# Five units' convolution taps on TensorE, floors under squared norms moved, and a new order of issue in a fused attention and expert block

## The chip, the cores and the metric

The kernel runs on 1 core of a Trainium2 chip. The metric is the device time of one execution in microseconds (us), as the median of several runs. The engines are named as the profile names them: PE is TensorE (matmuls), PEld its weight loads, DVE is VectorE, ACT is ScalarE, POOL is GpSimd, and SP is the queue from which nearly all transfers are issued.

## The reference, cut to what matters

The input `x` has 8 sequences of 512 tokens with 128 features in f32. Four sublayers follow each other, each with a layer norm before it and an addition after it:

```python
x = x + attn_a(layernorm(x))   # short convolution, delta rule, 16 heads of 8
x = x + ffn(layernorm(x))      # 8 experts, two chosen for each token   ("f")
x = x + attn_b(layernorm(x))   # linear attention with elu + 1          ("b")
x = x + ffn(layernorm(x))      # the same experts again                 ("g")

# in attn_a
q = silu(short_conv(x @ Wq.T, conv_q))      # 4 taps along the tokens; k and v alike
q, k = l2norm(q), l2norm(k)                 # x / max(sqrt(sum(x * x)), 1e-6)
v_new = (v_t - k_t S) * beta_t;  S = S + k_t v_new;  o_t = q_t S    # token by token
o = o * rsqrt(mean(o * o) + 1e-6) * o_norm_w;  out = o @ Wo.T
# in ffn
probs = softmax(x @ Wg); the two largest, divided by their sum, weigh
relu(x @ W1[e]) @ W2[e]
```

## The kernel before

**Units.** The 512 tokens are cut into eight units of 64 tokens (times 8 sequences, so 512 rows). Each unit goes through the sublayers in turn, and the units overlap. `prepare(c)` does unit c's layer norm, projections, convolution, norms and the solve of four tokens at a time; `recurring` runs the delta rule over all units, 16 steps for each, with four VectorE operations in a step (`pj`, `factors`, `terms`, `st`); POOL forms the outputs (`po`) and `ending(c)` normalizes them and sends them through DRAM (`sco`, `oT`). `moe` runs the experts for f and g, `linear_attention` and `attend` run b. In the profile the first sublayer's tiles end in `_a`, and the others in `_f`, `_b` and `_g`. "f1" below is the expert sublayer f of unit 1.

**The order.** Each part is a Python generator that yields the name of the engine that it needs next, or an event to wait for. A planner (`Weaver`) keeps a modelled clock for each engine and always lets that part issue whose work is longest behind, corrected by `FAVOURED` and by one number for each part in `OFFSETS`. What comes out is one fixed order of instructions on each engine, and each engine works strictly in that order, PE's matmuls among them. Where the planner sees a gap on PE, `keep_busy` puts bf16 matmuls into it whose result nobody reads; line 1950 issues them and the profile calls them `busy`.

**The convolution.** `TAPS_ON_PE = 4`: for units 0 to 3, `convolved(s)` (s is q, k or v) uses four f32 matmuls with weights `wc[s]` in which the taps are folded into the projection. The profile shows two matmul records for each f32 matmul. For units 4 to 7 it uses one matmul with the plain weights `wa`, a copy to `cv` and a multiplication on ACT, three `scalar_tensor_tensor` on DVE, and two small `halo` copies on POOL. The first unit of that kind also needs three small matmuls into `pl`.

**What shares a buffer.** The folded weights `wc` lie in the space of the last three experts' weights (`resident[5]` to `resident[7]`). So `loading_later_weights` must wait:

```python
if TAPS_ON_PE and e >= NE - 3:
    yield fired("projected", TAPS_ON_PE - 1, e - (NE - 3))
```

The loads of experts 5 to 7, and the matmuls that centre their first weights (`s_cw_w` in the profile), can come only after unit 3's convolution.

**Linear attention.** In `attend`, POOL forms outer products of keys and values in the one buffer `kv`; PE then sums them along the tokens (`s_pc_b`), DVE multiplies by the queries (`qs_b`) and reduces (`nd_b`).

**Routing.** `moe` finds the largest and the second largest logit with `first_of_largest`, one after the other, then `relative` computes the two weights with a tanh on ACT, then the weights go to `cb`. From there `spread` writes them to DRAM, and each expert reads its row back as `wt_xsT`, which POOL multiplies with the tokens before `s_ph` starts.

**Floors.** A squared norm is raised to at least 1e-12 directly after it is computed: on POOL in `norms_of` (units 0 to 4), on DVE in `near_norms` (k of unit 0, and units 5 to 7).

Of the kernel before, what the change touches and what calls it, by code (L numbers as in the profile page):

```python
# [19 lines left out]
P = 128  # L20
# [17 lines left out]
TURNED = 1  # L38
# [3 lines left out]
TAPS_ON_PE = 4  # L42
# [4 lines left out]
ADDED_ON_DVE = (4,5,6,7)  # L47
NEAR_NORMS = (5,6,7)
# [5 lines left out]
TURNED_IN = (0,7)  # L54
# [13 lines left out]
PASSES = ()  # L68

FAVOURED = {  # L70
    ("b", 0.0): 1475, ("b", 1.0): -605, ("b", 2.0): 408, ("b", 3.0): -1141, ("b", 4.0): 1159, ("b", 5.0):
    -397, ("b", 6.0): -3095, ("b", 7.0): -2237, ("b", 7.5): -2071, ("beside",): 1509, ("ending",): 696,
    ("f", 0): 1839, ("f", 1): 922, ("f", 2): 673, ("f", 3): -941, ("f", 4): 1648, ("f", 5): 1050, ("f", 6):
    -1587, ("f", 7): 767, ("f", 7.5): -2892, ("g", 0.0): 1576, ("g", 1.0): 901, ("g", 2.0): 357, ("g", 3.0):
    7212, ("g", 4.0): -253, ("g", 5.0): -2424, ("g", 6.0): -246, ("g", 7.0): 1986, ("g", 7.5): -2626,
    ("outputs",): 7, ("prepare", 0): -904, ("prepare", 1): -3306, ("prepare", 2): 224, ("prepare", 3):
    -1571, ("prepare", 4): -839, ("prepare", 5): -16, ("prepare", 6): 680, ("prepare", 7): -2427, ("recur",
    0): 3219, ("recur", 1): -6342, ("recur", 2): -2844, ("recur", 3): 482, ("recur", 4): -2744, ("recur",
    5): -1405, ("recur", 6): 1064, ("recur", 7): -724, ("values",): 149, None: -1498,
# [4 lines left out]
    -5735, -5206, -179, -62, -5753, 0, -6219, -6323, 29, -6838, 1464, 2372, 2338, -2, 1277, -3446, -3136,  # L84
    2417, -3137, -2112, -3119, -3650, -311, 76, 1, 3, -3, 77, -342, -7970, 977, -20, -4091, 3665, -19, 806,
    -4343, -4621, -4648, -4379, 711, 806, -5289, 1734, 1900, 1275, 623, -5269, -420, -380, -832, -1479, 50,
    -758, -790, 125, -3620, 585, -553, 237, 2322, 2064, -5521, 501, -5381, -5928, -3498, -40, 2563, 4086,
    10628, -5495, 782, 11097, 2142, 524, -2998, -175, 1440, -9862, 334, 747, 94, -5047, -6796, 307, 308,
    -1787, -402, -3506, -63, -187, 265, -2927, -6059, -6411, -6618, 0, -4528, -6371, -6553, -6091, -5056,
    263, -538, -1107, -6503, -6983, -6, -6510, -36, -961, -967, 294, 389, -6742, -8230, -142, -7747, -8737,  # L90
    -7250, -7254, -7665, -422, 1935, 282, -996, -6683, -9031, 177, 1221, 466, 360, -7342, 552, -8817, -42,
    -7371, 101, 1699, 247, 245, 186, -7410, 57, 713, -5151, 127, -91, -80, -5933, 56, -6006, -6402, 412,
    -6116, -445, 35, 2434, -4925, -4928, -4874, -938, 1079, 406, -7960, 775, 519, -186, -183, -6551, -7752,
    -7695, -8113, 429, 2079, 1870, 73, 72, 717, 130, -428, -37, 347, 2267, 385, -69, 3340, -640, -367, 165,
    -831, -1483, 0, 486, -5539, -200, -199, -399, -34, 2547, -7582, -106, -2671, 11037, 1388, 1383, 1120,
    -962, 17, -1270, -6162, -175, -5673, 211, 50, -7246, -2444, -7484, -2599, -386, 24, -1456, -1295, -1542,
    449, 95, 3319, -2490, -5181, -17, 250, 1245, 968, 926, -3459, -1, -51, -7241, -6288, -40, -5786, 456, 0,
    2, -7292, 471, -361, -79, -6239, 1121, 209, 228, 171, -490, -335, -1339, -4313, -4533, -173, -162,
    -1885, -4676, -5235, -6460, -342, -6601, -6575, 266, 235, 4646, 4647, 78, -899, -7489, 388, -348, 4,
    2051, 1488, -3366, -170, -1594, -5834, -4738, -590, -6081, 2703, 771, 806, 2101, -1052, -4471, -334,  # L100
    10046, 384, -6869, -6546, 10224, -8058, 323, -1252, 463, 8950, 0, -8361, 1480, -113, -361, -8416, -9767,
    -47, -200, -9523, 27, -8517, -60, 66, -8349, -229, -9575, -9613, 177, 0, -516, 2087, 1808, 1102, -3472,
    -3462, -3444, -261, -48, -604, -199, 8924, -1499, -2626, 0, -5333, -68, 0, -3882, -1964, 1388, 1387,
    -3692, -5022, -5065, -555, 136, 6558, 1420, 1897, 1801, 9994, 299, 277, 324, -41, 8082, 391, 7156, 7157,
    -5841, -322, -1273, -5351, 627, 9366, -2233, -2747, 1391, 674, -7825, -11438, -30, 775, 2023, 1821,
    -1660, -376, -7698, 679, -3112, 1424, -5849, 0, -55, 151, -899, 680, -7529, -8147, 148, 896, 1077, 914,
    339, 108, 425, -1456, -5019, -1472, -477, 2580, -4207, -3854, -4163, -8696, -1145, -4645, -48, -435,
    -49, -441, -2007, 528, -6603, 2721, 2590, 71, 790, 1764, 678, -1104, -11, -8403, -631, -307, -17, 8979,
    -26, 111, 125, -3643, 387, 709, -7661, -6188, -1529, 52, -267, -2256, -1638, -163, -7464, -7718, -7716,
    -1060, 1984, -7251, 341, -416, 74, 246, 826, 0, -1331, 114, -9262, 817, -794, -1132, -4670, 22, 677,  # L110
    -1102, -247, -991, 5324, 1460, 7056, -68, 22, -4777, -5911, -267, -245, 0, -5384, 611, 1441, -3227,
    -3228, 7000, -4910, -4927, 8594, 7076, 656, 8970, 534, 0, -414, -452, 8696, 199, -1793, 526, 7399,
    -2385, -2142, -2082, 703, 601, -344, 673, 889, 675, -225, 700, 0, 1159, -2605, -52, 1613, 16, -121, 10,
    3158, 128, 131, -45, -73, 1613, -6492, -6728, -6847, 1627, -162, 2762, 283, 57, -585, 605, 1, -6681,
    -6644, -7468, 1614, -1785, -6492, 3296, -2793, 740, 1374, 1438, -5170, -5140, 909, 2571, -5016, 298,
    -5165, -4644, -50, -42, -4475, 2, 294, -85, -2740, -6839, 226, 1693, -57, 3901, -15, 128, 27, -353,
    1777, -988, 548, -1117, 51, -5550, -5713, 147, 12, -34, -4251, 1589, 1915, 47, -3918, 1053, 111, -9287,
    183, -73, -1509, -1272, -1576, 1611, -436, 1, 5846, -1241, -112, 1631, -1205, 1597, 150, -2745, -3535,
    2377, 2411, 1644, 1676, -1215, 1575, -4452, 8420, 702, -792, 816, 406, 430, 763, 8525, 846, -158, 8634,
    8574, 7499, -111, 1400, 1450, 1002, 8654, -2038, 769, 762, 607, 2855, 6551, -97, -90, -87, 5399, 647,  # L120
    -2965, 11537, -1025, 26, 1690, -128, 1901, -2876, -579, -1637, -1629, 2367, 1239, 1591, 19, 1583, 1724,
    11913, 9792, -979, -5647, 234, 2469, -6345, 305, -458, 202, 495, 2179, 331, -2292, 9691, 1045, 6, 9790,
    35, -5846, 323, 577, 1291, 9691, -58, -97, 118, -5, -4, 615, -5886, 76, -98, -106, -3895, 613, 2012,
    -4473, 833, 614, 2011, -59, -171, -3273, -3336, -3353, -3, -4885, 1032, 10012, 4, 9990, -8535, 13, -26,
    -426, 9852, -8409, 100, -8705, 1140, -1782, -3, -354, -197, -1938, -335, 9717, -197, 9802, 2602, -4020,
    6594, -4069, 2798, 3058, 2, -79, -78, 391, 1966, 1709, 200, 8716, 1885, 10615, 11418, 3662, 9797, 2272,
    1035, 2099, 0, 1824, 10195, 9823, 10532, 9755, 10009, 1333, 1142, -251, 8119, 297, 296, 41, 749, 4723,
    747, 1875, 2107, 724, -124, 453, 7278, 3607, 3799, 273, 3441, 3113, -3692, -398, -3768, -334, -3765,
    -3766, -582, -412, 9876, -382, 1211, 10712, -1001, 93, -1201, 9799, -302, 9584, 9796, 780, 9701, -580,
    1068, 9799, -828, -878, 2215, 2732, -4744, 3104, 2677, 2684, 2623, 238, -387, -153, 2284, -614, 2072,  # L130
    231, 2027, -4996, -71, 30, 457, -4797, 384, -249, 4030, 2190, -5523, 4173, 1217, 3083, 1929, -714, 605,
    676, -732, -321, -57, 3956, 733, 11526, -7059, -800, 1502, 239, -723, -808, -318, -541, 8037, -8544, 15,
    -4952, -5089, -5252, -4993, 2029, -304, -831, -5698, -69, -6182, -350, -409, 2461, 257, -282, -7155,
    -5747, 0, -11360, 2325, 2107, 2122, 386, -5700, -3106, -1352, 0, 0, -1541, 372, -1538, -3081, -1573,
    -1435, -66, 3013, -2727, -4066, -895, -131, -4357, 2917, -4077, -498, 0, -3157, -80, -404, -3201, -3374,
    0, 1576, 1292, 11286, -3695, -3696, 11437, 2265, 10445, 11425, 0, 3814, -3061, -6147, -44, -59, 400,
# [331 lines left out]
def duration(key, op, args, kw):  # L468
# [12 lines left out]
    if key == "ACT":  # L481
        table = TABLE_OF.get(args[2]) if op == "activation" else None
        scale = args[2] if op == "mul" else kw.get("scale", 1.0)
        more = (0.19 if "bias" in kw else 0.0) + (0.0 if isinstance(scale, float) else 0.08)
        return key, 0.2 + more + n * 0.76e-3, 0.1, table
# [1523 lines left out]
```

## Time and profile before

| what | value |
|---|---|
| median of 3 runs | 792.27 us (791.22 to 794.27) |
| the profiled execution | 790.81 us, span 789.1 us |
| PE busy | 758.7 us, 96% of the span |
| of that, `busy` matmuls (line 1950) | 52.7 us in 195 |
| DVE, ACT, POOL busy | 560.8, 504.7 and 446.0 us |

A PE that is busy is not always doing useful work: the `busy` matmuls count as busy. In a list of instructions or of a chain the first two numbers are the start and the duration in us. In a table of stages, each engine's busy time in the stage is followed by its number of instructions; the last three columns are the granted PE clock as a share of full speed, the share of time in which the DMA engines moved data, and GB/s.

### The profile page before, as it was taken

What the parts mean: (1) busy time and instruction counts of PE and PEld (TensorE: products, weight loads), DVE (VectorE), ACT (ScalarE), POOL (GpSimd) and SP (SyncE); (2) the same over time, 40 slices, a digit from 0 to 9 for tenths busy, and PEclk for the clock granted to TensorE, in tenths of its full rate; (3) what the DMA queues carried; (4) which work ended last, traced back from release to release, by engine and by line L of the source; (5) the groups of instructions that cost most, each with busy time, mean ns of one, the idle gap of its engine ahead of it and who ended that gap; (6) DMA issues with size and microseconds to landing.
All of it is one profiled execution on the core that took longest, in us unless ns stands there. A gap on an engine that the chain in (4) does not pass through costs nothing.

```text
span 789.1 us, 11578 instructions
## 1 busy us (share of the span) xinstructions
PE 758.7 (96%) x3383; PEld 384.7 (49%) x3383; DVE 560.8 (71%) x1429; ACT 504.7 (64%) x1388; POOL 446.0 (57%) x609
## 2 busy tenths in 40 slices
PE   8888899997999999999999999999999999999997
PEld 4344454553435434544444435453444456644475
DVE  1689898978997698899999799798557145342310
ACT  5765767688877865678676875773664445643352
POOL 1244447659586495775586664877736606735331
PEclk9999899998999999999999999999999999999999
DMA  1451426105233311214132132232112211321121
GB/s 46 118 133 42 123 63 183 45 23 148 69 97 80 98 56 55 81 55 126 54 111 96 34 102 78 82 106 67 42 41 81 60 28 48 108 69 44 37 60 34
DMA packets 82392, 59.67 MB, mean 76 GB/s; under 512 B 48152, under 2 KB 64152, under 8 KB 82328
## 3 DMA queue, kind: packets, MB, share of 16 engines
q1 hardware_dynamic: 81608, 58.64, 25.8%
q8 instruction: 27, 0.44, 0.2%
q10 hardware_dynamic: 720, 0.28, 0.2%
q14 instruction: 37, 0.30, 0.1%
HBM read 46.52 MB, written 12.39 MB: 75 GB/s over the span
## 4 chain that ended last, share of the span: by engine, by line
PE 78%; DVE 11%; ACT 6%; issue 2%; DMA 2%; POOL 1%; SPq 0%; DVEq 0%; ACTq 0%; POOLq 0%
PE s_ph_f L454 14%; PE y_py_f L454 13%; PE s_ph_g L454 13%; PE y_py_g L454 12%; PE s_pc_b L454 5%; PE s_pp_a L454 4%; PE s_pp_b L454 2%; PE busy L1950 2%; PE s_pu_b L454 2%; DVE st L454 2%; PE s_pS_b L454 2%; DVE W L454 1%; ACT squares L454 1%; DVE pj L454 1%; DVE terms L454 1%
## 5 line engine op out<-in xcount | busy, mean ns | idle before, releaser
L454 ACT ACTIVATE hT_g<-s_ph_g 128x512 f32<-128x512 f32 (+1 forms) x144 | 79.0, 552 | 95.5 <-PE s_ph_g L454 94.5
L454 PE MATMUL y_py_f<-hT_f,resident 128*128 128x512 f32 (+1 forms) x288 | 134.3, 555 | 0.3 <-ACT hT_f L454 0.2
L454 PE MATMUL s_ph_f<-wt_xsT_f,resident 128*128 128x512 f32 (+1 forms) x288 | 132.1, 554 | 1.9 <-POOL wt_xsT_f L454 1.1
L454 PE MATMUL y_py_g<-hT_g,resident 128*128 128x512 f32 (+1 forms) x288 | 133.3, 553 | 0.3
L454 PE MATMUL s_ph_g<-wt_xsT_g,resident 128*128 128x512 f32 (+1 forms) x288 | 131.0, 553 | 0.3 <-POOL wt_xsT_g L454 0.2
L454 ACT ACTIVATE hT_f<-s_ph_f 128x512 f32<-128x512 f32 (+1 forms) x144 | 78.7, 550 | 50.9 <-PE s_ph_f L454 49.4
L454 POOL TENSOR_TENSOR wt_xsT_g<-wt_xsT_g,xn_xnT_g 128x512 f32<-128x512 f32 (+1 forms) x69 | 79.0, 1166 | 37.0 <-DMA wt_xsT_g<-scw_g 26.7
L454 POOL TENSOR_TENSOR po<-st,kq 128x256 f32<-128x256 f32 x128 | 93.8, 763 | 3.3 <-DVE st L454 2.7
L454 POOL TENSOR_TENSOR kv_b<-ph_b,v 128x1152 f32<-128x1152 f32 x32 | 69.2, 2176 | 39.8 <-ACT v L454 27.1
L454 POOL TENSOR_TENSOR wt_xsT_f<-wt_xsT_f,xn_xnT_f 128x512 f32<-128x512 f32 (+1 forms) x69 | 79.4, 1168 | 17.5 <-DMA wt_xsT_f<-scw_f 17.4
L454 DVE TENSOR_TENSOR qs_b<-s_pc_b,ph_b 128x360 f32<-128x360 f32 (+1 forms) x96 | 50.4, 551 | 46.2 <-PE s_pc_b L454 45.5
L454 PEld LDWEIGHTS y_py_f<-hT_f,resident 128*128 128x128 f32 x288 | 50.6, 190 | 47.2 <-issue 40.4
L454 PEld LDWEIGHTS s_ph_f<-wt_xsT_f,resident 128*128 128x128 f32 x288 | 50.4, 190 | 47.4 <-issue 31.6
L454 PEld LDWEIGHTS y_py_g<-hT_g,resident 128*128 128x128 f32 x288 | 50.9, 190 | 44.1 <-issue 35.6
L454 PEld LDWEIGHTS s_ph_g<-wt_xsT_g,resident 128*128 128x128 f32 x288 | 50.9, 190 | 43.7 <-issue 32.0
L454 DVE TENSOR_REDUCE st<-terms 128x64 f32<-128x320 f32 x128 | 61.4, 480 | 12.3 <-ACT terms L454 6.0
L454 DVE TENSOR_REDUCE factors<-pj 128x32 f32<-128x288 f32 x128 | 58.4, 456 | 6.2 <-ACT factors L454 2.5
L1950 PE MATMUL busy<-ones 128*128 128x512 bf16 x195 | 52.7, 411 | 9.5 <-ACT o L454 3.4
L454 DVE TENSOR_TENSOR pj<-st,factors 128x256 f32<-128x256 f32 x128 | 53.4, 417 | 4.7 <-ACT factors L454 1.8
L454 DVE TENSOR_TENSOR terms<-factors,kt 128x256 f32<-128x256 f32 x128 | 53.7, 419 | 4.2 <-ACT vn L454 1.1
L454 ACT COPY terms<-st 128x64 f32<-128x64 f32 x128 | 39.6, 309 | 25.0 <-DVE st L454 23.8
L454 POOL TENSOR_TENSOR pq<-y_a,y_a 128x128 f32<-128x128 f32 x32 | 21.1, 685 | 46.2 <-ACT squares L454 23.1
(270 smaller groups left out, 1336.1 us busy)
## 6 DMA issues: line engine op xcount, KB each, us to landing
wt_xsT_f<-scw_f SPq DMA_DIRECT2D x55, 256.0 KB
wt_xsT_g<-scw_g SPq DMA_DIRECT2D x55, 256.0 KB
scr<-y_a SPq DMA_DIRECT2D x24, 256.0 KB
qk<-scr SPq DMA_DIRECT2D x16, 256.0 KB
x_a<-in_x_dram SPq DMA_DIRECT2D x16, 128.0 KB
vv<-scr SPq DMA_DIRECT2D x8, 256.0 KB
sco<-on SPq DMA_DIRECT2D x8, 256.0 KB
oT<-sco SPq DMA_DIRECT2D x8, 256.0 KB
```

The costliest lines, as they stand in the source:

```text
L454: r = call(*args, **kw)
L1950: nc.tensor.matmul(pt, ones, ones.unsqueeze(1).to_broadcast([P, 4, P]), start=True, stop=True)
```

## The change

The change has these parts:

1. The folded taps lie in the buffer `kv` of the outer products, and `TAPS_ON_PE` goes from 4 to 5. Experts 5 to 7 no longer wait for unit 3. Instead, the first unit's `attend` waits until unit 4's convolution matmuls are done before it takes `kv`.
2. Unit 4 uses 12 f32 matmuls for its taps in place of three matmuls and the ACT, DVE and POOL operations. The three `pl` matmuls move to unit 5.
3. The floor under q's squared norm goes into the operation of `ending` that adds the mean square, with `max` in the place of `mult` and the scales changed around it. The floor under k's norm in `near_norms` moves behind the square root in `back`. Five operations of POOL and seven of DVE go, and four of DVE come.
4. `relative` is started as soon as the second largest logit is known, beside the search for its place.
5. Unit 0's denominators of b lie in PSUM, in one of the five general banks.
6. The planner: other estimated durations, ten more planning passes (`PASSES`), new `FAVOURED` and `OFFSETS`. All engines get another order of instructions.

Other new branches (`STATES_ON_PE`, `KEYS_ON_POOL`, `QUERIES_ON_POOL`) are switched off by empty tuples. `TURNED` is written in another way and says the same as before.

```diff
-TAPS_ON_PE = 4
+TAPS_ON_PE = 5
+BURST = NE - 3
...
-PASSES = ()
+PASSES = ((1, 0.0, {}), (9, 0.1, {}))
...
 FAVOURED = {
...
 OFFSETS = (
...
@@ duration
-        more = (0.19 if "bias" in kw else 0.0) + (0.0 if isinstance(scale, float) else 0.08)
+        more = (0.1 if "bias" in kw else 0.0) + (0.0 if isinstance(scale, float) else 0.06)
         return key, 0.2 + more + n * 0.76e-3, 0.1, table
     if key == "POOL" and ALU.pow in args:
-        return key, 1.05, 0.1
+        return key, 0.4 + n * 0.16, 0.1
     if key == "POOL":
-        return key, 0.2 + n * (1.72e-3 if n > 512 else 2.0e-3), 0.1
+        if op == "tensor_copy":
+            return key, 0.16 + n * 1.3e-3, 0.1
+        return key, 0.18 + n * (1.73e-3 if n > 512 else 2.15e-3), 0.1
...
@@ merged
-    wc = [resident[NE - 3 + s].rearrange("p (k d) -> p k d", k=4) for s in range(3)]
+    kv_ = const.tile([P, 2, NH, V1, HD], F32, name="kv")
+    taps = kv_.rearrange("p w h e d -> p (w h e d)")[:, 0 : 12 * D].rearrange("p (s k d) -> p s k d", s=3, k=4)
+    wc = [taps[:, s] for s in range(3)]
...
-    kvs = held_in(1, [P, 2, NH, V1, HD], "kv")
+    kvs = Slots(weaver, None, None, "kv", 1, [kv_])
...
@@ loading_later_weights
-            if TAPS_ON_PE and e >= NE - 3:
-                yield fired("projected", TAPS_ON_PE - 1, e - (NE - 3))
...
                 sp.dma_start(resident[e][:, to], by)
+                if e >= BURST and to.stop < 2 * NF:
+                    weaver.moves(-LANDS)
...
@@ norms_of
-            yield "POOL" if CLAMP_ON_POOL else "DVE"
-            (pool if CLAMP_ON_POOL else dve).tensor_scalar(
-                nrm[:, s], nrm[:, s], ATT_A_EPS * ATT_A_EPS, None, ALU.max
-            )
+            if s:
+                yield "POOL"
+                pool.tensor_scalar(nrm[:, s], nrm[:, s], ATT_A_EPS * ATT_A_EPS, None, ALU.max)
...
@@ near_norms
-            yield "DVE"
-            dve.tensor_scalar(nrm[:, s], nrm[:, s], ATT_A_EPS * ATT_A_EPS, None, ALU.max)
...
@@ back
             act.activation(ri, nrm[:, 1], AF.Sqrt, scale=4.0)
+            if c == 0 or c in NEAR_NORMS:
+                yield "DVE"
+                dve.tensor_scalar(ri, ri, 2.0 * ATT_A_EPS, None, ALU.max)
...
@@ ending
-        act.activation(so, o, AF.Square)
+        act.activation(so, o, AF.Square, scale=(ATT_A_EPS * HD * HD) ** -0.5)
...
-        dve.scalar_tensor_tensor(rms, nrm[:, 0], ATT_A_EPS * HD * HD, rms, ALU.mult, ALU.add)
+        dve.scalar_tensor_tensor(rms, nrm[:, 0], ATT_A_EPS * ATT_A_EPS, rms, ALU.max, ALU.add)
...
-        act.activation(rms, rms, AF.Sqrt, scale=1.0 / HD)
+        act.activation(rms, rms, AF.Sqrt, scale=ATT_A_EPS * HD)
...
@@ moe
+        def relative(m1, m2):
...
+        def first_of_largest(p, k):
+            m = near(nb) if k else row(f"m{k}")
+            yield "DVE"
+            dve.tensor_reduce(m, p, AX.X, ALU.max)
+            if k:
+                scales["weights"] = spawn(relative(m1, m))
...
-        m2 = yield from first_of_largest(lg2, 1)
...
-        yield from relative()
+        yield from first_of_largest(lg2, 1)
+        yield scales["weights"]
...
@@ attend
         adding = spawn(elus())
+        if c == 0:
+            yield from all_of([fired("projected", TAPS_ON_PE - 1, s) for s in range(3)])
         kv = yield from kvs.take(n)
...
-        dn = yield from dns.take(n)
-        if c > 0:
+        if c == 0:
+            of_dn = yield from banks.take(f"dn_{n}")
+            dn = of_dn[:, 0 : 2 * NH].rearrange("p (i h) -> p i h", i=2)
+        else:
+            dn = yield from dns.take(n)
...
```

## The prediction

> **What bounds the kernel now.** I read the page's first two parts, then PE's time by stages, then the chain that ended last around the one stage that loses time, then the timeline and the single tiles.
>
> ```profile
> span 789.1 us, 11578 instructions
> PE   8888899997999999999999999999999999999997
> PEclk9999899998999999999999999999999999999999
> ```
>
> PE is full from about 200 us to the end and granted full speed there, except in the last slice. The other engines never come near. But a busy PE may be running `busy` matmuls, so I take four stages, first with all instructions, then line 1950 alone:
>
> ```profile
> 0.00:123.00 123.00, 108.92 (x527) 57.43 (x528) 91.15 (x242) 80.27 (x236) 46.11 (x95) 0.97 0.35 92
> 123.00:200.00 77.00, 68.74 (x326) 37.24 (x325) 65.26 (x153) 60.96 (x182) 56.20 (x84) 0.96 0.33 93
> 200.00:760.00 560.00, 556.75 (x2425) 271.87 (x2424) 403.27 (x1033) 353.44 (x946) 336.14 (x420) 1.00 0.24 71
> ```
>
> ```profile
> 0.00:123.00 123.00, 37.14 (x144) 14.70 (x144) 0.97 0.35 92
> 123.00:200.00 77.00, 11.22 (x36) 4.01 (x36) 0.96 0.33 93
> 200.00:760.00 560.00, 1.56 (x5) 0.49 (x5) 1.00 0.24 71
> ```
>
> The second column of numbers is PE's busy time. PE's lost time (stage less busy, plus `busy` matmuls) is 14.1 + 37.1 = 51.2 us before 123 us, 8.3 + 11.2 = 19.5 us up to 200 us, and only 3.3 + 1.6 = 4.9 us in the 560 us after. So work taken from DVE, ACT or POOL after 200 us is worth nothing, work added to PE there costs its full time, and a gain must come from the first 200 us. The worst stretch there is 160 to 192 us:
>
> ```profile
> 160.00:192.00 32.00, 24.89 (x149) 14.54 (x148) 26.23 (x70) 27.15 (x78) 23.19 (x37) 0.89 0.30 86
> ```
>
> Of 32 us, 7.1 are idle and 9.0 more (the same window of line 1950) are `busy`: 16.1 us lost. The chain of waits shows who holds it:
>
> ```profile
> 173.14 0.77 DVE s_pp_a L454
> ...
> 179.23 0.48 ACT cv_a L454
> 179.70 0.56 ACT s_pp_a L454
> ...
> 183.90 1.28 ACT L454
> 185.19 0.63 ACT mn_b L454
> ...
> 186.12 0.47 ACT v L454 x2
> 186.59 0.04 issue
> 186.63 5.07 PE busy L1950 x12
> 191.70 2.58 PE s_ph_f L454 x6
> ```
>
> `cv_a` and `s_pp_a` on ACT and DVE are unit 4's convolution. They stand in ACT's and DVE's order ahead of what unit 0's b needs (`mn_b`, `v`). Then PE, which goes in order, does 12 useless matmuls before it starts the experts of f1, although POOL's timeline has the first two of their inputs finished at 181.5 us (179.00 plus 2.53).
>
> **The change part by part.** Sums are made against the profiled execution, 790.81 us (the span and 1.7 us around it). The median lies 1.46 us above it.
>
> *Taps of unit 4.* The tile's view prices what goes and comes:
>
> ```profile
> L454 PE MATMUL s_pp_a<-xnT_a,resident x96: 590/591/697, 11.5 to 117.2; 128*128 128x512 f32 x96
> L454 DVE SCALAR_TENSOR_TENSOR s_pp_a<-cv_a,cw,s_pp_a x36: 741/748/756, 172.3 to 462.3; 128x512 f32<-128x512 f32 x36
> L454 ACT COPY cv_a<-s_pp_a x12: 568/594/636, 168.3 to 457.4; 128x512 f32<-128x512 f32 x12
> L454 ACT ACTIVATE s_pp_a<-s_pp_a,cw x12: 634/670/757, 171.6 to 459.1; 128x512 f32<-128x512 f32 x12
> ```
>
> For one unit, 9 × 0.748 = 6.7 us leave DVE, 3 × (0.594 + 0.670) = 3.8 us leave ACT, and six copies of 0.21 us leave POOL; two copies of 0.21 us come to ACT. PE's records go from 6 to 24. Matmuls overlap, so I use their spacing: the chain has 22 of them in 9.54 us, 0.434 us each. The 18 more cost 7.8 us of PE, less than the 16.1 us lost in this stretch. On the chain between 168 and 187 us the pieces that go are 3.8 us of DVE `s_pp_a` (1.60 + 0.75 + 0.67 + 0.65 + 0.14) and 1.6 us of ACT (0.57 + 0.48 + 0.56): 5.4 us. That is the most that `v` can gain. The new wait takes a part back. POOL's first `kv_b` starts at 186.98 us; behind it in POOL's order stand f1's next input, the outputs `po`, and through them PE's `s_pc_b`. The last of unit 4's matmuls now ends at 177.3 us; with 7.8 us more at the same place the taps end at 185.1 us, which lets `kv_b` come only 1.9 us sooner. If the planner starts the taps earlier, in the 3.4 us lost between 123 and 160 us and in the gaps at 172 and 178, the full 5.4 us remain. I take the middle, **-3.7 us** (-5.4 to -1.9). The cover is the lost time: a tap that runs after 192 us costs its 0.43 us, 7.8 us for all. The three `pl` matmuls (0.78 us) move to unit 5, where PE has no slack: **+0.8 us**.
>
> The clock matters to the cover. The window above was granted 0.89, and its 12 `busy` matmuls took 0.42 us each, where 20 others, at 60.6 us in the chain, took 0.22 us each. The Trainium skill, "TensorE: Matmul & The Clock Gate", Part 1, says that PE falls to half rate after an idle window of about 3.4 us and needs as long a busy one to come back. This speaks against the change: by this rule, taps issued just after a gap run at half rate for up to 3.4 us, which delays `kv_b` by up to 1.7 us, and the sum would be 785.2 us in place of 783.5.
>
> *Experts' loads.* Nine issues on SP of about 0.46 us (4.1 us) leave 116 to 146 us and come before 85 us, where SP also issues `scr`, `qk` and `nrm` of units 0 to 2. Late there is only unit 1's preparation, whose recurrence starts when DVE has finished `W` at 78.3 us, so a transfer late by one issue (0.46 us) is hidden by that; without this cover it costs as much. At the old place the first `wt_xsT_f` took 4.15 us to land, with DMA engines busy 64% of 110 to 130 us; if the load on them delays it, up to 2 us are won, but other transfers share that stretch, and I take nothing. The centring of those three weights, six matmul records, stood twice on PE's chain at 0.43 us (144.46 and 152.31) and once before it; all can use lost time now: 3 × 0.43 = **-1.3 us**.
>
> *Routing.* In f0, before which PE has nothing to do, the five operations after the second search stand at 115.44 to 117.07 us on DVE, 1.6 us, with the tanh between them. They go beside the search: **-1.6 us**. They still use DVE, so 0.8 us (five of 0.16 us) is the least that could be lost again. In the other 17 routings PE has other work; nothing.
>
> *Floors.* POOL saves 5 × 0.37 us and DVE a net 3 × 0.2 us. The only place on the chain is unit 0's k: 0.20 us at 25.09 us goes before the root and 0.20 us comes behind it. Nothing, 0.8 us either way if each of the four new floors were on the path. *Unit 0's denominators* in a bank: three small operations of some 0.8 us in all hold one of five banks; nothing, or 0.8 us if a matmul waits for it.
>
> *Order.* It cannot be read from the diff, so I bound it by the holds that an order can remove. One is f1's start: 191.7 less 181.5 is 10.2 us, of which 5.4 are counted above, so 4.8 us more. The other is on POOL, which sat idle for 7.5 us until 83.36 us before unit 1's `pq`, with unit 0's second correction `oc` behind it; all of f0 hangs on that. Together at most -12.3 us. An order can also make holds of this size, so the other end is +12.3 us. The planner's price for the small `pow` on POOL was 1.85 us with its extra 0.8 and is now 1.04 us, which is what the trace shows (1.04), so better aims speak a little for a gain. I take a quarter, **-3 us**.
>
> Sum: -3.7 + 0.8 - 1.3 - 1.6 - 3 = -8.8 us, so 782.0 us for the profiled execution and 783.5 us for the median. I say 783. With every part at its better end: -5.4 + 0.8 - 1.3 - 1.6 - 2 - 12.3 = -21.8 us, 770.5 us for the median.
>
> **Rivals.** *A: the taps run on a full PE (slower).* Unit 4's taps also need unit 3's `y` buffers back and room behind unit 0's output. If the new order starts them later than about 184 us (192 less 7.8), they run in the saturated part and `kv` waits for them as well; f1's matmuls cover that wait on PE, but nothing covers the taps: 7.8 + 0.8 - 1.3 = +7.3 us, 799.6 us for the median. For it: before, they start at 166.6 us, and f1's experts, ready at 181.5, may go ahead of them. Against: the 16.1 lost us lie exactly there.
>
> *B: no change.* The front moves by a few us and the taps eat it: for instance half of the taps uncovered (+3.9) against -3.7 + 0.8 - 1.3. That is -0.3 us, 792.
>
> *C: the new order also removes both holds.* -3.7 + 0.8 - 1.3 - 1.6 - 12.3 = -18.1 us, 774 us. For it: all lost time is in the front, 70.7 us. Against: f0 also waits for the first recurrences on DVE, which no part shortens.
>
> **How the numbers follow.** Two executions of this kernel may differ by 0.4% (791.2 to 794.3), so 0.5%, 4 us, is about what can be told from no change. The forecast (777 to 788, with its order term between 3 us worse and 6 us better) has a chance of 0.43, C 0.20, B 0.12 and A 0.25. Faster is the forecast and C, 0.63; same is B, 0.12; slower is A, 0.25. The range is 769 to 800: it takes in C, B and A's value, and leaves out the upper half of A's order term and the few orders better than C.
>
> **What would show it.** Right: 120 matmul records `s_pp_a<-xnT_a,kv`; 27 `s_pp_a` operations left on DVE; the lost time before 200 us down from 70.7 to about 54 us (8.8 won and 7.8 filled with taps), and from 200 to 760 us still near 5 us; f1's first `s_ph_f` ahead of 191.7 us by several us. For A: taps at 190 us or later, and lost time before 200 us not under 70 us. Wrong in another way: `kv_b` of unit 0 waiting long for PE's `s_pp_a`, lost time of PE appearing after 200 us, or a slower clock in the front.

## The result and the profile after

The changed kernel takes 795.06 us (median of 16 runs, 794.29 to 796.05), the kernel before 791.26 us (16 runs, 789.65 to 795.60). The ratio is 1.0042, with a 95% interval of 1.0030 to 1.0054: slower by 0.42%, just inside the 0.5% that the prediction called no change. The forecast was faster, 783 us. The profiled execution took 795.15 us with a span of 793.4 us, so 4.3 us more span than before.

The page's first parts look the same as before, with a PE that seems to be full:

```profile
span 793.4 us, 11511 instructions
PE   8898888998989999999999999999999999999997
PEclk9999999999899999999999999999999999999999
```

The three stages of the kernel after, first all instructions, then the `busy` matmuls alone (in this kernel line 2015 issues them):

```profile
0.00:123.00 123.00, 106.79 (x509) 55.41 (x510) 86.53 (x231) 81.82 (x248) 45.81 (x93) 0.99 0.37 99
123.00:200.00 77.00, 71.76 (x326) 36.49 (x323) 64.56 (x156) 61.05 (x172) 53.49 (x84) 0.99 0.32 93
200.00:760.00 560.00, 552.98 (x2389) 269.69 (x2391) 404.29 (x1012) 347.66 (x925) 336.13 (x409) 0.99 0.24 69
```

```profile
0.00:123.00 123.00, 35.08 (x134) 0.99 0.37 99
123.00:200.00 77.00, 3.29 (x14) 0.99 0.32 93
200.00:760.00 560.00, 0.38 (x1) 0.99 0.24 69
```

Made into lost time in the prediction's way (stage less busy, plus `busy` matmuls):

| stage, us | lost before | lost after |
|---|---|---|
| 0 to 123 | 51.2 | 51.3 |
| 123 to 200 | 19.5 | 8.5 |
| 200 to 760 | 4.9 | 7.4 |
| 760 to the end | 7.6 | 5.3 |
| sum | 83.1 | 72.5 |
| PE's useful time (span less lost) | 706.0 | 720.9 |

So 10.6 us of lost time did go, in the very stretch where the prediction had looked for them, and yet the span is 4.3 us longer, because PE's useful time grew by 14.9 us. The groups of instructions say by what: `s_pp_a` by 7.8 us (the taps, exactly as priced), `s_ph_f` by 3.5 and `y_py_f` by 2.1 us, although their 576 records are the same (in g the same two groups take 2.1 us less). Most of what f's records gained is a slower clock. The stage from 200 to 240 us shows it, first before, then after (the clock is the third number from the end):

```profile
200.00:240.00 40.00, 38.33 (x178) 15.76 (x177) 36.71 (x87) 29.53 (x76) 28.46 (x40) 1.00 0.28 80
```

```profile
200.00:240.00 40.00, 35.64 (x139) 16.49 (x140) 35.05 (x83) 27.62 (x70) 24.20 (x28) 0.88 0.27 81
```

PE's timeline of the kernel after names the waits there. The last column is PE's idle time ahead of a group, and who ended it:

```profile
193.14 1.12 PE L457 MATMUL y_py_f<-hT_f,resident 128*128 128x512 f32 x2 [0.33 <-ACT hT_f L457]
...
197.63 1.13 PE L457 MATMUL y_py_f<-hT_f,resident 128*128 128x512 f32 x2 [1.88 <-ACT hT_f L457]
199.83 2.08 PE L457 MATMUL s_po_a<-woa,oT 128*128 128x128 f32 x8 [1.08 <-ACT y_a L457]
201.70 1.91 PE L457 MATMUL s_ph_f<-wt_xsT_f,resident 128*128 128x512 f32 x2
...
223.15 2.08 PE L457 MATMUL y_py_f<-hT_f,resident 128*128 128x512 f32 x2 [2.58 <-ACT hT_f L457]
```

This is f1, and PE has little else to do than f1: four groups of its second matmuls wait for ACT's `hT_f`, 5.5 us in all, and two `s_ph_f` records take 1.91 us where two take 1.02 us at full clock. Four groups of two such records (`s_ph_f` or `y_py_f`) between 201.70 and 226.70 us take 7.5 us instead of 4.1. f1 itself starts sooner than before, as the prediction had hoped. First before, then after:

```profile
191.54 2.74 PE L454 MATMUL s_ph_f<-wt_xsT_f,resident 128*128 128x512 f32 x6
```

```profile
186.21 1.88 PE L457 MATMUL s_ph_f<-wt_xsT_f,resident 128*128 128x512 f32 x4
```

But its last step (`s_pty_f`) starts at 238.07 us, where it started at 234.37: f1 begins 5.3 us sooner and ends 3.7 us later. In the kernel before, b0 ran beside f1 (first outer products at 186.98 us). Here b0 comes 33 us later:

```profile
219.94 4.31 POOL L457 TENSOR_TENSOR kv<-ph_b,v 128x1152 f32<-128x1152 f32 x2
```

A part of this delay begins 110 us earlier, in PE's order:

```profile
97.98 10.47 PE L457 MATMUL s_pp_a<-xnT_a,kv 128*128 128x512 f32 x24
...
109.94 1.16 PE L457 MATMUL s_po_a<-woa,oT 128*128 128x128 f32 x8 [1.13 <-ACT y_a L457]
...
130.96 1.98 PE L457 MATMUL s_ph_f<-wt_xsT_f,resident 128*128 128x512 f32 x4 [0.46 <-ACT wt_xsT_f L457]
132.78 2.74 PE L457 MATMUL s_pp_a<-xnT_a,kv 128*128 128x512 f32 x6
...
138.08 7.14 PE L457 MATMUL s_pp_a<-xnT_a,kv 128*128 128x512 f32 x16
```

All of unit 3's taps now stand ahead of unit 0's output projection `s_po_a`, which came at 102.38 us before; the first `s_ph_f` of f0 follows at 130.96 us instead of 122.68; and unit 4's 24 tap records lie between the first and the second expert of f0. f0's last step (`s_pty_f`) starts at 187.93 us instead of 164.30.

POOL's order does its part. Before, it multiplies the first three of f0's rows from 127.71 us on; after, one at 138.64 us and three more from 141.38 us on, with work of the other units ahead of them. First before, then after:

```profile
127.71 3.75 POOL L454 TENSOR_TENSOR wt_xsT_f<-wt_xsT_f,xn_xnT_f 128x512 f32<-128x512 f32 x3 [1.09 <-DMA wt_xsT_f<-scw_f]
```

```profile
141.38 3.72 POOL L457 TENSOR_TENSOR wt_xsT_f<-wt_xsT_f,xn_xnT_f 128x512 f32<-128x512 f32 x3
```

So of the 33 us, 8.3 are there at f0's start, 23.6 at its last step, and the rest comes between that step and the outer products.

### The profile page after: what moved, and what is told of

Read it like the earlier page. It is cut to its first block, busy times and chain, and to the rows that moved or that the text cites. A ratio compares the mean times of both kernels' runs of the same rounds, so it can differ in the third digit from the quotient of the medians.

```text
span 793.4 us, 11511 instructions
## 1 busy us (share of the span) xinstructions
PE 760.2 (96%) x3355; PEld 385.0 (49%) x3355; DVE 559.8 (71%) x1417; ACT 504.5 (64%) x1384; POOL 444.2 (56%) x598
## 4 chain that ended last, share of the span: by engine, by line
PE 79%; DVE 9%; ACT 7%; issue 3%; POOL 2%; DMA 0%; DVEq 0%; ACTq 0%; POOLq 0%
PE s_ph_f L457 13%; PE s_ph_g L457 13%; PE y_py_f L457 13%; PE y_py_g L457 12%; PE s_pp_a L457 6%; PE s_pc_b L457 5%; ACT squares L457 3%; PE s_pp_b L457 2%; PE s_pu_b L457 2%; PE busy L2015 2%; PE s_po L457 1%; PE s_pS_b L457 1%; DVE st L457 1%; DVE factors L457 1%; DVE pj L457 1%
## 5 line engine op out<-in xcount | busy, mean ns | idle before, releaser
L457 PE MATMUL y_py_f<-hT_f,resident 128*128 128x512 f32 (+1 forms) x288 | 136.4, 560 | 5.5 <-ACT hT_f L457 5.5
L457 PE MATMUL s_ph_f<-wt_xsT_f,resident 128*128 128x512 f32 (+1 forms) x288 | 135.6, 564 | 1.7 <-ACT wt_xsT_f L457 0.5
L457 ACT ACTIVATE hT_f<-s_ph_f 128x512 f32<-128x512 f32 (+1 forms) x144 | 78.8, 551 | 62.8 <-PE s_ph_f L457 61.0
L457 POOL TENSOR_TENSOR kv<-ph_b,v 128x1152 f32<-128x1152 f32 x32 | 69.0, 2175 | 53.3 <-DVE ph_b L457 20.9
L457 PE MATMUL s_pp_a<-xnT_a,kv 128*128 128x512 f32 x120 | 54.1, 598 | 0.0
L457 DVE TENSOR_REDUCE nd_b<-qs_b 128x90 f32<-128x720 f32 (+1 forms) x48 | 45.4, 946 | 0.5
```

The lines of the kernel that those rows point to most:

```text
L457: r = call(*args, **kw)
```

## The experiments

The theory after the result: the taps and the relief (unit 4's operations that leave ACT, DVE and POOL) do about what was priced, but the new order puts preparation ahead of f0, and that costs more than both. The rival: the order is neutral and the taps themselves cost, since they do not hide. Each ratio below is to the kernel before on the same chips, with its 95% interval. Edits marked "untimed" keep the planner's clocks, so that the order of all else stays as it was.

### Two orders by three ways of unit 4's convolution

`before_taps_alone`: 18 more records on PE, none of unit 4's ACT, DVE and POOL operations, the order of before. The taps use the plain weights, so b0's wait for the buffer `kv` is not in it:

```diff
+                for k in range(3 if c == 4 else 0):
+                    nc.tensor.matmul(pp, wa[:, s * D : (s + 1) * D], xnT[:, :, k : k + CH], ...)
...
-                act.copy(cv[:, :, 3:], pp3)
+                emit(act, "ACT", "copy", cv[:, :, 3:], pp3)      # unit 4: untimed, nothing issued
```

> The kernel before with its order kept and only unit 4's convolution done as in the change: 12 tap matmuls (with the plain weights, so the values differ), no copy to cv, no multiplication on ACT, no additions on DVE, no halo copies. This is the prediction's term for the taps alone: 1.9 to 5.4 us faster than the kernel before, because the ACT and DVE work ahead of unit 0's b goes and PE has 16 us of lost time there. Rival 'full PE': up to 7.8 us slower. If POOL's kv or the bank holds f1 anyway: no change.

Measured: 794.18 us, ratio 1.0043 (1.0030 to 1.0057), so 3.3 us slower. PE's timeline of this kernel; line 1007 are the taps:

```profile
167.46 2.74 PE L1007 MATMUL s_pp_a<-xnT_a,wa 128*128 128x512 f32 x6
170.13 0.43 PE L454 MATMUL s_pm_b<-xn_xnT_b,wg 128*32 128x128 f32 x8
...
171.45 2.74 PE L1007 MATMUL s_pp_a<-xnT_a,wa 128*128 128x512 f32 x6
174.03 0.27 PE L454 MATMUL s_pm_b<-ident,narrow_mT_b 128*128 128x128 f32 x1
...
179.21 1.08 PE L454 MATMUL s_pp_b<-wb,xn_xnT_b 128*64 128x128 f32 x10
```

PE is idle or `busy` for 16.1 us in this stretch, but not at the place where the taps are issued. There b0's own small matmuls stand behind them: the second `s_pm_b` came at 168.96 us before and comes 5.1 us later, `s_pp_b` 4.5 us later, f1's first `s_ph_f` at 194.84 instead of 191.54 us. That last 3.3 us is the whole loss.

`before_unit4_work_off` leaves the same operations out and adds no taps:

> The kernel before, in which unit 4's 9 DVE, 6 ACT and 6 POOL operations of the convolution are left out and no taps come in their place (its taps of the three earlier tokens are thus missing); the order of all else is kept. It measures the gain side of the prediction's taps term by itself. The prediction: up to -5.4 us (786). What the kernel with the taps alone suggests (its lost time before 240 us fell by 6.0 us while 7.8 us of matmuls came, and it was 3.3 us slower): -1 to -2.5 us, about 789, since f1's first matmul waits for POOL's row product behind kv_b. If the relief is worth nothing: 791.

Measured: 788.42 us, ratio 0.9964 (0.9950 to 0.9978). The relief of ACT and DVE is worth 2.8 us. The difference of these two kernels, 5.8 us, is what 7.8 us of taps cost in the order of before.

`after_9_taps_less` does the same in the order of after (unit 4 keeps one matmul for each of q, k and v):

```diff
+                    if c == 4 and k:
+                        weaver.took(*duration("PE", "matmul", ...))      # untimed, nothing issued
+                        continue
```

> The changed kernel with its order kept, but unit 4's convolution uses 3 of its 12 tap matmuls (the second to fourth tap are left out, so 18 of 24 matmul records, 7.8 us of PE). Theory 'order' (the taps are covered, the loss is in how the new order stalls PE later): these matmuls ran at 132.8 to 145.1 us, when the rows of f0's experts were not ready before about 140 to 145 us, so 0 to 4 us faster than the changed kernel (791 to 795 us). Rival 'full PE' (the taps cost what they last): 7.8 us faster, about 787 us.

Measured: 794.19 us, ratio 1.0038 (1.0025 to 1.0050), 0.9 us less than after. There the taps are nearly free: without them PE waits for POOL's `po`, which stands in PE's order ahead of f0's second expert:

```profile
141.17 3.78 PE L457 MATMUL s_po<-po,ident 128*128 128x128 f32 x16 [3.96 <-POOL po L457]
```

f0's last step comes at 187.26 us and b0's `kv` at 219.32 us, 0.6 to 0.7 us sooner than in after. So it is not the taps that make f0 and b0 late there.

`after_unit4_by_operations` undoes the taps part in the order of after: one matmul, and the ACT, DVE and POOL operations put in where the planner's clocks have room.

> The kernel after with the taps part undone: unit 4's convolution is done by one matmul and ACT, DVE and POOL operations again (and three pl matmuls come to unit 4), put in where the planner's clocks have room; the order of all else is that of after. With before (791), before_taps_alone (794), before_unit4_work_off (788) and after_9_taps_less (794) this fills a table of two orders by three ways. If the taps part costs 3 us in this order too: about 792. If the new order is what costs (its own reading: without taps and without operations it stands 5.8 us above the order of before), the operations are late here and hold DVE's and ACT's order: 795 to 798, and the taps part by itself gains 0 to 3 us in this order.

Measured: 801.17 us, ratio 1.0116 (1.0094 to 1.0138). A part of it is my way of putting them in, since PE waits for the bank of the third `pl` matmul behind ACT:

```profile
143.28 0.62 PE L495 MATMUL s_pl_a<-late,wa 128*128 128x24 f32 x2 [4.52 <-ACT halo L495]
```

So the number is an upper end. The table (medians in us):

| | nothing for the taps | operations | taps |
|---|---|---|---|
| order of before | 788.4 | 791.3 | 794.2 |
| order of after, with the other parts | 794.2 | 801.2 or less | 795.1 |

The runs were made on several chips, and differences in this table are good to about 1 us. Read across, the taps part costs 2.9 us in the old order (3.3 by its own pair) and gains in the new one, by 6.1 us at most. Read down, the new order with the other parts costs 5.8 us with nothing in the taps' place, up to 9.9 us with the operations and 0.9 us with the taps (nothing by the ratios, 1.0042 and 1.0043).

So the two costs do not add up. From the kernel with nothing for the taps (788.4), the taps alone cost 5.8 us, the new order with the other parts alone costs 5.8 us, and both together 6.6 us. Neither the theory nor the rival holds alone: the taps do not hide in the old order, and the new order has room for them but costs as much by itself.

### What in the order costs

`before_f0_behind_unit3` takes one step of the new order into the old one (`replay` holds the old order, and `deferred` keeps the part's place in it):

```diff
+        if c == 0 and weaver.replay is not None:  # unit 0's output projection
+            for s in LAST_OF_3:                   # (0, 1, 2)
+                weaver.deferred.append(weaver.stream.key)
+                yield fired("projected", 3, s)    # unit 3's convolution is issued
         yield from add_projected(xt, oTs[c][:, lo : lo + nb], woa, f"a{n}")
```

> The kernel before, in which unit 0's output projection s_po_a, and with it all of f0, waits in PE's order until unit 3's convolution is issued, as in the kernel after; the order of all else is kept. Theory (what the new order costs is f0's later start: f0's first s_ph_f at 131 us in after and 123 in before, so that b0 comes late and f1 runs alone, bound by ACT): f0 starts 4 to 9 us later and the kernel takes 3 to 8 us longer, 794 to 799. Rival (f0's start is covered, and the new order loses time by other things, in f1 itself): 790 to 792.

Measured: 798.58 us, ratio 1.0091 (1.0072 to 1.0109), 7.2 us slower. `s_po_a` comes at 116.16 us, and f0 starts where it starts in after:

```profile
130.93 1.98 PE L478 MATMUL s_ph_f<-wt_xsT_f,resident 128*128 128x512 f32 x4 [0.24 <-ACT wt_xsT_f L478]
```

b0's `kv_b` follows at 194.99 us, 8.0 us later than before, and of f0's 8.2 us 7.2 reach the end. In this kernel nothing takes f0's place on PE; its lost time before 200 us rises from 70.7 to 78.8 us. In after the taps of units 3 and 4 take it, so the lost time falls, but the delay of b0 is there all the same. This run shows what such a delay costs in the old order; how much of the cost in after is due to it, and how much to POOL's order or to the other parts, was not tried.

`before_offsets_zero` and `after_offsets_zero` plan each kernel with zeros for all of `OFFSETS`:

> The kernel before planned with all numbers in OFFSETS at zero: another order of the same instructions. It sizes the order term: the prediction bounded it at 12.3 us either way by two holds. If an order can cost more than such holds, this one is over 12 us slower, 805 to 850.

> The kernel after planned with all numbers in OFFSETS at zero. Beside before_offsets_zero it compares the two kernels' parts where neither order is fitted to them, though with other planning passes and durations: if the parts (taps, loads, routing, floors) gain by themselves, this is the faster of the two by some us; if the parts cost, the slower.

Measured: 939.5 and 913.75 us (two runs each). The same instructions in another order take 148 us longer, so two holds are no bound for what an order can cost (this one is fitted to nothing, so it does not measure what the change's order costs). That the changed kernel is 26 us faster here fits parts that help by themselves, but its planning passes and durations differ too, so it shows no more than that.

### What held f1 in the kernel before

The prediction read 10.2 us between 181.5 us (two rows of f1 finished on POOL) and 191.7 us (first `s_ph_f`) as a hold, with 12 `busy` matmuls at its end. `before_12_fillers_less` leaves these 12 out, untimed:

> The kernel before without the 12 busy matmuls that stand on PE ahead of f1's first expert (186.6 to 191.7 us). If they hold f1: PE starts f1 when DVE has freed its bank at 186.8 us, 4.9 us sooner, and the kernel is up to 4.9 us faster. Rival 'clock': PE was at about half clock there, and without the busy matmuls f1's own matmuls run slow until it recovers, so most of it is lost again: 0 to 2 us.

Measured: 793.56 us, ratio 1.0033 (1.0020 to 1.0045), 2.7 us slower. PE's and then POOL's timeline of this kernel:

```profile
190.51 5.12 PE L454 MATMUL s_ph_f<-wt_xsT_f,resident 128*128 128x512 f32 x6 [6.08 <-POOL wt_xsT_f L454]
```

```profile
187.06 2.17 POOL L454 TENSOR_TENSOR kv_b<-ph_b,v 128x1152 f32<-128x1152 f32 x1 [0.96 <-DVE ph_b L454]
189.19 1.27 POOL L454 TENSOR_TENSOR wt_xsT_f<-wt_xsT_f,xn_xnT_f 128x512 f32<-128x512 f32 x1
```

The rows that were ready are those of experts 1, 3 and 2; f1 begins with expert 0, and that row stands on POOL behind the first `kv_b`. The `busy` matmuls held f1 by 1.0 us at most, and they paid for it: after 6.08 us of idle time the six records take 5.12 us, where they took 2.74 us behind the `busy` matmuls. The rule of the Trainium skill ("TensorE: Matmul & The Clock Gate", Part 1) that PE falls to half rate after an idle window of about 3.4 us agrees with this pair; some gaps of 2.6 us do not fit it, as the last section shows.

`before_row_0_first` lets the rows of experts 0 and 2 of f1 change places; the planner then sees no gap, and the 12 `busy` matmuls go:

```diff
-        turned = {e: spawn(expert(e)) for e in range(4)}
+        turned = {e: spawn(expert(e)) for e in ((2, 1, 0, 3) if name == "f1" and weaver.replay is not None else range(4))}
```

> The kernel before, in which the rows of experts 0 and 2 of f1 change places: POOL multiplies expert 0's row where it multiplied expert 2's (182.1 us), and expert 2's behind the first outer products kv_b (189.1 us). The planner then sees no gap ahead of f1 and the 12 busy matmuls there go by themselves. Theory (f1's first matmul waits for that one product on POOL, which stood behind kv_b, and not for the busy matmuls): the first s_ph_f of f1 starts at 184 to 186 us instead of 191.5, in place of busy and idle time, and 3 to 5 us are won: 786 to 788 us. Rival (some other input of f1 or of b0 comes last anyway, and the next wait takes the place of this one): within 1 us of the kernel before, with PE idle a little later.

Measured: 791.01 us, ratio 0.9994 (0.9983 to 1.0005). No gain, as the rival said. PE's timeline of this kernel:

```profile
187.07 5.20 PE L477 MATMUL s_ph_f<-wt_xsT_f,resident 128*128 128x512 f32 x6 [2.62 <-DVE ph_b L477]
192.82 1.12 PE L477 MATMUL y_py_f<-hT_f,resident 128*128 128x512 f32 x2 [0.55 <-ACT hT_f L477]
```

f1 now waits for its bank (`ph_b` on DVE frees it), then runs at half clock, then waits for ACT. It starts 4.5 us sooner, and its first `y_py_f` comes only 1.3 us sooner. Behind the hold stood two more of nearly the same length.

`before_k_taps_in_the_gap` uses what the first table says: of unit 4's three convolutions, only k's goes to taps, with the folded weights in the buffer `kv` as in the change, and its three extra matmuls stand where PE waits for f1.

```diff
             halves(pb, heads, src.rearrange("p (b t) -> p b t", b=NB))
+            if c == 4 and i == 0:                 # behind the norm of q, at 184 us
+                for k in range(3):
+                    nc.tensor.matmul(of["pq"], wc[1][:, k, :], xnT[:, :, k : k + CH], start=False, stop=k == 2)
```

> The kernel before, in which of unit 4's three convolutions only the last one (k) is done by taps, with the folded weights in the buffer kv as in the change; the three added matmuls stand behind s_pn_a at 184 us, where PE waits for f1, and ACT loses 1.3 us and DVE 2.2 us of work ahead of b0's v. The order of all else is that of before. Theory (taps are free only where PE waits, and the relief of ACT and DVE ahead of v is what gains): f1's first matmul at 189.5 to 190.5 us instead of 191.5, 1 to 2.5 us won, 788.5 to 790. Rival (the relief of unit 4's last part alone moves nothing, since b0's v waits for PE's s_pp_b): 791.

Measured: 790.14 us, ratio 0.9983 (0.9966 to 0.9999): 1.3 us faster than before, just clear of the noise, and 4.9 us faster than after. PE's timeline; line 901 are the taps:

```profile
184.06 2.84 PE L901 MATMUL s_pp_a<-xnT_a,kv 128*128 128x512 f32 x6
186.74 2.75 PE L1968 MATMUL busy<-ones 128*128 128x512 bf16 x12
189.92 2.84 PE L454 MATMUL s_ph_f<-wt_xsT_f,resident 128*128 128x512 f32 x6 [0.43 <-POOL wt_xsT_f L454]
```

The taps stand where PE was idle, the `busy` matmuls behind them run at full clock (2.75 us, 5.07 before), and f1 starts 1.6 us sooner. The gain is that of the taps and of the relief together.

`before_k_taps_and_row_0` has both edits:

> The kernel before with both: k's taps of unit 4 in the gap ahead of f1, and rows 0 and 2 of f1 changed (the busy matmuls ahead of f1 go by themselves). Alone they gave 790.1 (ratio 0.9983) and 791.0 (0.9994). In the first, f1's first matmul waits for the row behind kv_b (189.9 us, after 2.8 us of busy matmuls); in the second it starts at 187.1 us at half clock, after a gap. Theory: here it starts at about 187 us directly behind the taps, so at full clock, and the two gains add up to 2 to 3 us: 788 to 789.5. Rival (ACT's order ahead of f1's first hT_f, with a table load, ends at 190.5 us anyway): no more than k's taps alone, 790.

Measured: 792.30 us, ratio 1.0014 (1.0001 to 1.0027). They do not add up. f1 starts at 186.52 us at nearly full clock, and its first second matmul stands at 192.00 us behind ACT:

```profile
192.00 1.13 PE L477 MATMUL y_py_f<-hT_f,resident 128*128 128x512 f32 x2 [2.34 <-ACT hT_f L477]
```

Why it is slower than k's taps alone is not settled: its profiled execution took 790.31 us, as little as theirs, so the trace does not show the difference.

### f1 in the kernel after

`after_no_squares_b0` leaves out the four squares with their sums on ACT for b0's layer norm (the variance of b0 is a constant there), which stand ahead of f1's `hT_f` at 194.6 to 196.8 us:

> The changed kernel with its order kept, without the four squares on ACT for unit 0's variance in b (194.6 to 196.8 us; a constant takes their place). Theory 'order and clock': PE waits there for a relu that stands behind them on ACT; without them PE idles some 2 us less, keeps its clock, and f1's matmuls at 200 to 206 us run at full speed: 2 to 5 us faster than the changed kernel. Rival: the next wait (the table load and y_a behind it) takes the place: 0 to 1 us.

Measured: 793.99 us, ratio 1.0039 (1.0026 to 1.0051). The clock from 200 to 240 us rose from 0.88 to 0.96, and PE's idle time there from 4.4 to 5.8 us. f's records took 2.4 us less, and f1's last step started at 234.16 us instead of 238.07. Yet the time fell by 1.1 us at most (0.3 by the ratios): the next waits, for ACT and then for POOL's `pq`, took the place. This row has the longest of them; its two records run at full clock, behind a gap as long as that of after:

```profile
220.75 1.12 PE L457 MATMUL y_py_f<-hT_f,resident 128*128 128x512 f32 x2 [2.58 <-ACT hT_f L457]
```

`after_12_fillers_more` puts 2 and 10 `busy` matmuls into f1 to keep the clock:

> The kernel after, with 12 more busy matmuls on PE in f1, ahead of the second matmuls number 6 (2) and 10 (10), where PE stood idle 0.7 us at 211 us and 2.6 us at 220 us. Theory (the idle time behind ACT's hT_f lowers the granted clock, 0.91 between 220 and 240 us, and slows the matmuls behind it): the clock there is 1.00 and 1 to 2 us are won, 793 to 794 us. Rival (the matmuls behind the gap wait for ACT again, so that the clock is of no use): no gain, 795, or up to 1 us slower where a busy matmul stands in the way.

Measured: 795.39 us, ratio 1.0050 (1.0031 to 1.0068), no gain. The experiment did not do what it was meant to: the free bank was freed by ACT as late as `hT_f` itself.

```profile
222.60 2.32 PE L1531 MATMUL busy<-ones 128*128 128x512 bf16 x10 [2.57 <-ACT hT_f L457]
```

They ran behind the gap of 2.57 us, not in it. The `y_py_f` behind them started at 224.76 us instead of 223.15, and the full clock only made up for that: the next `y_py_f` starts at 226.48 us here and at 226.54 us in after. So this run does not say what a full clock is worth in this stage; `after_no_squares_b0`, which had nearly one, gained 1.1 us at most. What both runs show is that f1 is bound there by the chain through ACT.

### The floors

`before_floors_alone` moves the floors as in the change, in the order of before, with each new DVE floor directly behind ACT's root in the order of issue; `before_floors_ahead_of_use` puts it directly ahead of the reciprocal that reads it.

```diff
             act.activation(ri, nrm[:, 1], AF.Sqrt, scale=4.0)
+            if c == 0 or c in NEAR_NORMS:                                          # floors_alone
+                nc.vector.tensor_scalar(ri, ri, 2.0 * ATT_A_EPS, None, ALU.max)
...
             yield "DVE"
+            if c == 0 or c in NEAR_NORMS:                                          # floors_ahead_of_use
+                nc.vector.tensor_scalar(ri, ri, 2.0 * ATT_A_EPS, None, ALU.max)
             dve.reciprocal(ri, ri)
```

> The kernel before with the floors moved as in the change, in the same order. The prediction costs them at nothing, 0.8 us either way at most: 790 to 792 us. Rival: one of the four new floors behind the root stands on the path of a recurrence and costs more than 1 us.

Measured: 794.25 us, ratio 1.0038 (1.0026 to 1.0050), 3.0 us slower, which I had not expected. The group of the four floors:

```profile
L1062 DVE TENSOR_SCALAR s_near_a<-s_near_a 128x64 f32<-128x64 f32 x4 | 0.9, 233 | 6.5 <-ACT s_near_a L454 6.5
```

They take 0.9 us, and DVE stands still for 6.5 us ahead of them, since in their place it is there before ACT has made the root. All that is queued behind them on DVE waits too.

> The kernel before with the floors as in the change, but each new floor in DVE's order directly ahead of the reciprocal that uses it, not directly behind ACT's root. If the 3.0 us of before_floors_alone came from DVE standing still for the root (6.5 us of idle time before the four floors, where the reciprocals of before waited 1.9 us in all), this kernel is within 1 us of before: 790 to 792. Rival (four more operations of 0.23 us on the path to W, and the scaled squares, cost by themselves): 793 or more.

Measured: 791.02 us, ratio 0.9998 (0.9980 to 1.0016). The group of the four floors here:

```profile
L1065 DVE TENSOR_SCALAR s_near_a<-s_near_a 128x64 f32<-128x64 f32 x4 | 0.9, 233 | 2.0 <-ACT s_near_a L454 1.9
```

The floors are free if they stand where their input is nearly ready. How DVE's 6.5 us reach the end is not shown: PE's idle time between 240 and 500 us is 3.9 us in the first of these kernels and 1.2 us in before, but 3.3 us in the second one too, whose profiled execution took 793.67 us. In the changed kernel DVE waits 3.0 us ahead of its four floors, and what that costs there was not tried.

## Why the prediction was wrong, step by step

**Two terms failed: the order (-3 us) and the cover of unit 4's taps (within -3.7 us).** Their costs do not add up, so the runs do not split the loss between them in one way. With nothing in the taps' place, the new order cost 5.8 us (with the loads, the routing, the floors and the denominators, which stayed in) and the taps then 0.9. In the old order, the taps cost 5.8 us and the new order then 0.9. Either way 6.6 us stand against a relief of 2.8 us.

**The order.** Two things were wrong in the term. It took its size from two holds, and a hold says only what may be won there, not what another order may lose elsewhere; the zero offsets show 148 us, where the prediction's other end was 12.3. And both holds went in the changed kernel without a gain. f1 started 5.3 us sooner and ended 3.7 us later, with waits for DVE, ACT and POOL behind the one that went. On POOL, unit 0's `oc` no longer stands behind unit 1's `pq`, but `o` then waits for DVE, and unit 0's outputs leave for DRAM (`sco`) at 95.47 us, before at 95.54. What the new order moved was f0's start, from 122.7 to 131.0 us; in the old order, such a move alone costs 7.2 us. That this is also what costs in the changed kernel is likely, but not shown.

**The taps of unit 4.** The price on PE, 7.8 us, was right to the tenth. The cover was wrong: lost time in a stretch is no cover for a matmul that stands at a fixed place of an in-order queue. In the old order 5.8 of the 7.8 us came through; k's taps, put into the gap itself, were a small gain. The relief was half as large, 2.8 us instead of 5.4, as work taken off the chain let the next chain come forward: f1's first `s_ph_f` then waits for its row on POOL, at 189.27 us. In the new order the taps did hide (0.9 us), but in a place where PE would have waited for POOL.

**The clock** was named as what speaks against the change, with 1.7 us for taps after a gap. It slowed other matmuls: f's records took 5.5 us more of PE's time, 3.4 us of it in four groups of f1 between 201.70 and 226.70 us. That is not what it cost: where most of this slow clock was gone, the kernel gained 1.1 us at most. In the old kernel the slow clock had fallen mostly on `busy` matmuls (20 of them in 6.22 us at 95.64 us, 12 in 5.07 us at 186.63 us).

**Routing (-1.6 us).** The operations that can go beside the search are four on DVE, not five (115.44 to 117.07 us before). f0's routing on DVE, from `m_f` to `cb_f`, took 11.6 us (116.00 to 127.59) instead of 9.1 us (108.87 to 117.93). The change allows the four beside the search, but in f0 the order leaves them behind it (124.18 to 127.29 us), with the recurrence's operations between all steps; for 1.95 us of the time DVE waits for ACT's `o` ahead of one of these. From unit 0's output projection to f0's first `s_ph_f` it is 0.7 us longer than before, so nothing was won there.

**Floors (0)** was right in the old order, with the condition that the prediction did not see: in the wrong place they cost 3.0 us. **The loads and the centring (-1.3 us)** and **the denominators (0)** were not tried alone and lie within the order's 5.8 us; the last nine loads are issued at 90.5 to 100.0 us, not before 85. The three `pl` matmuls (+0.8 us) were not tried alone either.

**What would show it** came out mixed. 120 records `s_pp_a<-xnT_a,kv` and 27 of DVE's `s_pp_a` are there; the lost time before 200 us fell to 59.8 us, not to 54; from 200 to 760 us it rose to 7.4. f1's first `s_ph_f` came at 186.21 us, ahead of 191.7 by several us, and was no sign of a gain. Two signs of being wrong in another way were there: more lost time after 200 us and a slower clock, though in f1 and not in the front. Rival A had the sign and the wrong place: unit 4's taps ran from 132.8 to 145.2 us, long before 190. Rival B, no change, holds the measured time by its own bound of 0.5%.

## What to carry to other kernels

- On an engine that goes in order, idle time covers new work only if it lies between the same two instructions. Before pricing an addition at nothing, name the instruction behind it and who waits for that one.
- Lost time of the busiest engine can fall while the kernel gets slower: PE was filled with preparation, and the chain that feeds the rest (f0, then b0) came later. A matmul stage can also start sooner and end later, as f1 did. Follow the first chain that everything hangs on before the share of busy time.
- When a wait goes, look for the next one in every queue that the stage uses. Here PE, POOL, DVE and ACT each held f1 within a few microseconds.

## What the runs showed of the hardware that I had not expected

- Half clock came after shorter gaps than the prediction had reckoned with, but not always: the length of a gap does not decide it. In after, 2.58 us of idle time ahead of 223.15 us were followed by two records in 2.08 us, at a granted clock of 0.50 from 223 to 225 us. In `after_no_squares_b0` the same 2.58 us ahead of the same matmuls were followed by two in 1.12 us, and in `after_12_fillers_more` 2.57 us by ten `busy` matmuls in 2.32 us, at a clock of 1.00. In the old order, 2.62 us ahead of 187.07 us, with gaps of 1.70 and 1.54 us in the 10 us before, were followed by six records in 5.20 us (2.74 at full clock). In `before_unit4_work_off`, 2.17 us with shorter gaps before them were not followed by a slow clock:

```profile
185.36 2.75 PE L1960 MATMUL busy<-ones 128*128 128x512 bf16 x12 [2.17 <-ACT v L454]
```

- Matmuls with no use can be worth more than their time: 12 of them, 5.07 us of PE, left out cost 2.7 us.
